# A routed mixture of experts dealt in two halves of the sequences, the first half's blocks between the steps of the second half's routing

## The chip, the cores and the metric

The kernel runs on one core of a Trainium2 chip. The metric is the device time of one execution in microseconds (us); the median over several runs counts. An engine's clock, where it is shown, is the TensorE clock granted by the throttle, as a share of full speed.

## The reference

Two decoder layers, six sublayers one behind another, each of the form x = x + f(layernorm(x)): attention, retention over a context, a mixture of experts; then attention with a rotation and a codebook, multi-query attention over the same context, and a second mixture of experts. x holds 32 sequences of 128 tokens of 256 floats, all in float32. The change is in the last sublayer:

```python
def _L1_ffn_ref(X, routing_W, expert_bias, sW1, sb1, sW2, sb2, rW1, rb1, rW2, rb2):
    E = 8
    K = 2
    ...
    shared = jax.nn.silu(X @ sW1 + sb1) @ sW2 + sb2
    logits = jnp.einsum('btd,ed->bte', X, routing_W) + expert_bias
    activation = jnp.sqrt(jax.nn.softplus(logits))
    top_vals, top_idx = jax.lax.top_k(activation, K)
    ...
    hdn = jax.nn.silu(jnp.einsum('nd,edh->enh', Xf, rW1) + rb1[:, None, :])
    y = jnp.einsum('enh,ehd->end', hdn, rW2) + rb2[:, None, :]
    routed = jnp.einsum('ne,end->nd', cf, y).reshape(B, T, d)
    return shared + routed
...
x = x + _L1_ffn_ref(_layernorm(x, axis=-1), ...)
```

Every token has a shared expert and its best 2 of 8 experts, each 256 to 128 to 256, weighted by the root of the softplus of their logits.

## The kernel before

The 128 tokens of a sequence lie on the 128 partitions. The 32 sequences stay in SBUF as x and are worked in 8 groups of 4 (r0 to r7 below are the routing objects of groups 0 to 7). The stages follow each other: A (attention), B (retention), C (first mixture), D with E (the second layer's two attentions, in 46 steps numbered -13 to 32, about 10 us each once the pipeline is full), a tail that ends the routing of the last mixture, F (its blocks), and the collecting of their results.

*Dealing by tables.* The routed expert work is done on sorted rows. For each group, `RouteF.norm` normalises x into a tile `f_h` (three buffers), `turn` transposes it, `choose` makes the logits, `rank` (`Dispatch.choose`) finds the two best experts and counts how many tokens each expert got so far, `place` works out each token's two rows in a table in HBM, `g_xs`, that has a region of 33 x 128 rows for each of the 8 experts, and `store` sends f_h's rows there: eight scatters a group, on POOL's queue (L329). A row carries its token's number with it. The regions are cleared ahead of that, in stage B, so that unwritten rows are marked. When all counts are known, `Dispatch.finish` (L362) works out by small operations on DVE which expert each block of 128 rows belongs to and where it starts. Blocks never cross an expert's region, so 64 full blocks' worth of rows need up to 71 blocks.

*The shared expert.* `hidden` (L596), `turn_shares` (L604), `shared` (L614, L618) of the same objects add the shared expert and the weighted output bias to x; `share` and `root` make the weights of the two experts (`r_wt`, on POOL, L584).

*What lies where.* In stage E a step works one sequence's scores on PE, with the reduction `e_pad` (L1423) on DVE, and carries the routing of earlier groups along at fixed lags. The routing of groups 0 to 4 is stored within the steps, together with the shared expert of groups 0 and 1. All the rest, the stores of r5, all of r6 and r7, `finish` and the shared expert of groups 2 to 7, is the tail (L1562 to L1601).

*Stage F.* It loads the experts' weights on SP (L1614, 2 MB), then works the 71 blocks: `read` fetches 128 rows from g_xs at an address held in a register (SP queue, issued 9 blocks ahead, 12 buffers), `turn` transposes them (L1635), `up` (L1645), `turn_hidden` (L1654) and `down` (L1660) are the expert, with copies from PSUM on DVE (L1650, L1665) and on ACT, `address` works out on DVE where each row's result belongs (L433, L438; `g_to` and `g_toi`, eight buffers), and `send` scatters the 128 result rows into a second table, `g_ys` (L329, POOL). A step of the loop holds turn of block j+4, up of j+3, turn_hidden of j+1, down of j and the address of j+2. On PE and SP the order of the code is kept as written; on the other engines a scheduler orders the instructions.

*Collecting.* After the loop 16 fetches (SP, L457) of 512 KB each bring the results of two sequences back, `collect` adds them on DVE with their weights (L466, four operations a fetch), and `store` writes the finished x on ACT's queue (L1693, 256 KB).

Of the kernel before, what the change touches and what calls it, by code (L numbers as in the profile page):

```python
# [22 lines left out]
F32 = mybir.dt.float32  # L23
# [19 lines left out]
NBLK = 2 * B + E - 1  # L43
# [3 lines left out]
REGION = (B + 1) * P  # L47


W = dict(r=D + 4, g=D + 2)  # L50
# [16 lines left out]
class K:  # L67
# [150 lines left out]
    def table(self, name, pool):  # L218

        self.tables[name] = (  # L220
            pool.tile([E * REGION, W[name]], F32, name=f"{name}_xs", tag=f"{name}_xs"),
            pool.tile([(NBLK + 2 * B) * P, D], F32, name=f"{name}_ys", tag=f"{name}_ys"),
        )

    def clear(self, name, e, behind=None):

        to = self.tables[name][0][e * REGION : (e + 1) * REGION, :].rearrange("(n p) w -> p n w", p=P)
        empty = self.empty[:, 0 : W[name]].unsqueeze(1).to_broadcast([P, REGION // P, W[name]])
        inst = self.nc.sync.dma_start(out=to, in_=empty).ins
        self.order(inst, behind)  # L230
# [18 lines left out]

class Dispatch:  # L250
# [5 lines left out]
    def __init__(self, k, name, p1, p2):  # L256
        nc = k.nc
        self.k, self.nc, self.p1, self.p2 = k, nc, p1, p2
        self.use(name)
        self.tri = self.tile([P, P], "tri")  # L260
        nc.sync.dma_start(out=self.tri, in_=k.ins["before"])
        consts = self.tile([P, E + NBLK + 2 * B + 1], "consts")
        nc.sync.dma_start(out=consts, in_=k.ins["cconst"])
        o = [0, E, E + NBLK, E + NBLK + B, E + NBLK + B + 1, E + NBLK + 2 * B + 1]
        self.region, self.blocks, self.starts, self.part, self.tok = (
            consts[:, a:b] for a, b in zip(o, o[1:])
        )
        self.ones = self.tile([P, P], "ones")
        nc.vector.memset(self.ones, 1.0)

        self.cum = self.tile([P, B + 1, E], "cum")
        nc.vector.memset(self.cum[:, 0, :], 0.0)

        self.spare = self.tile([P, NBLK], "spare")
        nc.vector.tensor_scalar(self.spare, self.blocks, float(P), self.part, ALU.mult, ALU.add)
        self.wt = self.tile([P, 2, B], "wt")

        self.down = self.tile([P, E], "down")
        nc.vector.tensor_scalar(self.down, self.blocks[:, 0:E], -1.0, float(E), ALU.mult, ALU.add)

    def use(self, name):

        self.name = name
        self.xs, self.ys = self.k.tables[name]

    def tile(self, shape, name, dtype=F32):
        return self.p1.tile(shape, dtype, name=f"{self.name}_{name}", tag=f"r_{name}")
# [6 lines left out]
    def choose(self, g, v, h, behind=None):  # L294


        nc = self.nc
        down = self.down.unsqueeze(1).to_broadcast([P, GB, E])
# [4 lines left out]
        for n in range(2):  # L303
# [15 lines left out]
            h[:, :, D + 1], h[:, :, D], 0.0, self.tok[:, g * GB : (g + 1) * GB], ALU.mult, ALU.add  # L319
# [3 lines left out]
        for i in range(GB):  # L323
            b = g * GB + i
            nc.vector.tensor_add(self.cum[:, b + 1, :], self.cum[:, b, :], self.both[:, i, :])
# [11 lines left out]
    def place(self, g, h):  # L337
        nc = self.nc
        pp = self.k.bank([P, GB, E])
        nc.tensor.matmul(pp, lhsT=self.tri, rhs=self.both, start=True, stop=False)  # L340
        nc.tensor.matmul(pp, lhsT=self.ones, rhs=self.cum[:, g * GB : (g + 1) * GB, :], start=False, stop=True)
# [20 lines left out]
    def finish(self):  # L362
        nc = self.nc

        pn = self.k.bank([P, E])
        nc.tensor.matmul(pn, lhsT=self.ones, rhs=self.cum[:, B, :], start=True, stop=True)
        count = self.tile([P, E], "count")
        nc.vector.tensor_copy(count, pn)
        need = self.tile([P, E, B], "need")
        nc.vector.tensor_tensor(  # L370
            need, count.unsqueeze(2).to_broadcast([P, E, B]),
            self.starts.unsqueeze(1).to_broadcast([P, E, B]), ALU.is_gt,
# [5 lines left out]
        for e in range(1, E):  # L378
# [5 lines left out]
        over = lambda v: v.unsqueeze(1).to_broadcast([P, NBLK, M])  # L384
        done = self.tile([P, NBLK, M], "done")
        nc.vector.tensor_tensor(
            done, over(end[:, 0:M]), self.blocks.unsqueeze(2).to_broadcast([P, NBLK, M]), ALU.is_le
        )
        self.be = be = self.tile([P, NBLK], "be")
        nc.vector.tensor_reduce(be, done, AX.X, ALU.add)  # L390
        self.bei = self.tile([P, NBLK], "bei", I32)
        nc.vector.tensor_copy(self.bei, be)
        picked = self.tile([P, NBLK, M], "picked")
        nc.vector.tensor_mul(picked, done, over(nb[:, 0:M]))
        br = self.tile([P, NBLK], "br")
# [5 lines left out]
        bc = self.tile([P, NBLK], "bc")  # L401
# [3 lines left out]
        self.bri = self.tile([P, NBLK], "bri", I32)  # L405
        nc.vector.scalar_tensor_tensor(self.bri, be, float(REGION), br, ALU.mult, ALU.add)
        self.regs = {}

    def load_regs(self, b0):
        why = "counts of tokens, held to the table's range by min and max on the chip"  # L410
        n = min(NREG, NBLK - b0)
# [6 lines left out]
            self.bri[0:1, b0 : b0 + n], engines=[mybir.EngineType.SP], min_val=0, max_val=E * REGION - P,  # L418
# [33 lines left out]
    def fetch(self, g, yg, first=0, n=GB):  # L452

        rows = 2 * P
        o = NBLK * P + (g * GB + first) * rows
# [3 lines left out]
    def collect(self, g, first, n, yg):  # L459

        self.fetch(g, yg, first, n)
        for i in range(n):
            x = self.k.x[g][:, first + i, :]
            for r in range(2):
                b = g * GB + first + i
                self.nc.vector.scalar_tensor_tensor(x, yg[:, i, r, :], self.wt[:, r, b : b + 1], x, ALU.mult, ALU.add)  # L466
# [9 lines left out]
class Route:  # L476
# [4 lines left out]
    def __init__(self, k, g, pool, behind=None):  # L481
# [1367 lines left out]
```

## Time and profile before

| | us |
|---|---|
| median of 3 runs | 1663.46 (1662.84 to 1666.61) |
| the profiled execution | 1662.12 |
| its span on the core | 1660.3 |
| PE busy in the span | 1451.6 |
| DVE, ACT, POOL busy | 927.1, 603.8, 594.4 |
| first send of the blocks (L329, g_ys) | starts at 1531.06 |
| last send of the blocks | starts at 1621.05 |
| first sum of the collecting (L466) | starts at 1628.03 |

Times in the profile count from the start of the span. Busy time of an engine does not hold register, branch, semaphore and DMA-issuing instructions. In a line of a group of instructions stand the source line, the engine, the operation, what it writes and reads, its count, its busy time and the mean of one in ns, then the idle time ahead of it and what ended most of that. The time line of the scatters, of POOL, at the beginning of the blocks reads:

```profile
1510.69 3.30 POOL L584 TENSOR_TENSOR r_wt<-f_s,half 128x8 f32<-128x8 f32 x2
...
1531.06 1.06 POOL L329 DMA_INDIRECT g_ys<-f_yb,g_toi  x1 [15.88 <-DVE g_to L433]
```

That is start, length, engine, line and operation; the brackets give the idle time ahead of it and what released it.

### The profile page before, as it was taken

Reading aid. Unit: us, or ns where it says so; the run is one execution under the profiler, and the core shown is the slowest. Engines: PE = TensorE matmul, PEld = TensorE weight load, DVE = VectorE, ACT = ScalarE, POOL = GpSimd, SP = SyncE. Lnnn points to the kernel's source line nnn. Section 1 sums busy time; section 2 is a strip of 40 time slices with the busy share of each in tenths; the row PEclk is TensorE's granted clock in tenths of the full one; section 3 lists DMA queues with packets and bytes.
Section 4 is the critical chain, followed back from the end, with each engine's and each line's share of the span. In section 5 each row is a group of like instructions: output and inputs, shape, how many; then the busy total and the mean of one; then the engine's idle time right before and its main releaser. Section 6 shows DMA issues by size and latency. Waiting matters only on the chain.

```text
span 1660.3 us, 26693 instructions
## 1 busy us (share of the span) xinstructions
PE 1451.6 (87%) x9166; PEld 965.0 (58%) x9166; DVE 927.1 (56%) x2944; ACT 603.8 (36%) x1528; POOL 594.4 (36%) x615
## 2 busy tenths in 40 slices
PE   6999799999998469999999995799999999877990
PEld 4555567777776336666666664365555555545870
DVE  7566447777778533333333323635667775645766
ACT  2544333343444012222222221135565554432550
POOL 2110136677778511111111113102223443345770
PEclk9999999999999579999999997769999988878995
DMA  9991199911000731111111115400000000023658
GB/s 337 335 336 42 35 303 305 277 34 40 28 27 30 314 137 48 45 45 45 45 45 46 48 33 189 150 5 9 3 1 8 27 26 27 27 102 109 205 173 316
DMA packets 130615, 180.93 MB, mean 109 GB/s; under 512 B 11690, under 2 KB 110964, under 8 KB 128436
## 3 DMA queue, kind: packets, MB, share of 16 engines
q1 hardware_dynamic: 112020, 138.21, 27.1%
q0 software_dynamic: 12960, 35.60, 6.0%
q10 hardware_dynamic: 5504, 5.43, 1.0%
q8 instruction: 76, 1.25, 0.3%
q14 instruction: 55, 0.45, 0.1%
HBM read 68.88 MB, written 110.32 MB: 108 GB/s over the span
## 4 chain that ended last, share of the span: by engine, by line
PE 72%; DVE 10%; POOL 5%; DMA 5%; ACT 4%; issue 2%; ACTq 0%; SPq 0%; POOLq 0%; DVEq 0%
PE ps L1016 15%; PE ps L1036 7%; PE ps L159 6%; PE ps L649 3%; PE ps L1398 2%; PE ps L1438 2%; PE ps L1416 2%; PE ps L241 2%; PE ps L1645 2%; PE ps L1029 2%; PE ps L1660 2%; DMA f_yg<-g_ys 2%; PE ps L863 2%; PE ps L879 2%; PE ps L154 2%
## 5 line engine op out<-in xcount | busy, mean ns | idle before, releaser
L1016 PE MATMUL ps<-c_wx,c_xT 128*128 x568 | 268.2, 595 | 0.0
L329 POOL DMA_INDIRECT r_ys<-c_yb,r_toi x71 | 68.1, 960 | 356.8 <-DVE r_w L446 316.5
L1016 PEld LDWEIGHTS ps<-c_wx,c_xT 128*128 128x128 f32 x568 | 102.9, 191 | 73.5 <-issue 69.9
L1036 PE MATMUL ps<-c_wx,c_hid 128*128 x568 | 134.8, 380 | 0.9 <-DVE c_hid L1031 0.9
L1036 PEld LDWEIGHTS ps<-c_wx,c_hid 128*128 128x128 f32 x568 | 107.4, 190 | 47.2 <-issue 18.4
L150 POOL TENSOR_TENSOR b_rs<-b_var,mhalf 128x16 f32<-128x16 f32 x32 | 93.5, 2923 | 76.5 <-DVE b_var L897 76.4
L869 DVE TENSOR_TENSOR b_sim<-ps,b_decay 128x512 f32<-128x512 f32 x128 | 79.4, 683 | 72.3 <-PE ps L863 72.3
L1041 ACT ACTIVATE c_yb<-ps,r_w 128x256 f32<-128x256 f32 x71 | 33.7, 474 | 219.3 <-PE ps L1036 219.3
L1031 DVE COPY c_hid<-ps 128x512 f32<-128x512 f32 x71 | 49.0, 691 | 101.2 <-PE ps L1029 101.2
L1423 DVE TENSOR_REDUCE e_pad<-ps 128x4 f32<-128x512 f32 x128 | 82.2, 681 | 10.3 <-PE ps L1416 10.3
L150 POOL TENSOR_TENSOR ln_rs<-ln_ve,mhalf 128x4 f32<-128x4 f32 x40 | 40.8, 1023 | 129.9 <-DVE ln_ve L178 129.8
L329 POOL DMA_INDIRECT g_ys<-f_yb,g_toi x71 | 68.3, 961 | 38.6 <-DVE g_to L433 18.3
L176 DVE BATCH_NORM_STATS2 ln_st<-x 128x6 f32<-128x256 f32 x192 | 74.8, 406 | 9.5 <-DMA x<-in_x_dram 5.4
L1024 DVE TENSOR_TENSOR c_su<-ps,c_su 128x512 f32<-128x512 f32 x71 | 49.1, 692 | 55.1 <-PE ps L1016 55.1
L1468 POOL TENSOR_TENSOR x<-x,e_t 128x256 f32<-128x256 f32 x32 | 23.2, 726 | 155.9 <-DVE e_t L1463 155.8
L1439 ACT ACTIVATE e_e<-ps 128x512 f32<-128x512 f32 x128 | 67.4, 603 | 27.0 <-PE ps L1438 26.8
L329 POOL DMA_INDIRECT r_xs<-c_h,r_rowi x64 | 64.3, 1005 | 27.5 <-issue 14.3
L1022 ACT ACTIVATE c_su<-ps 128x512 f32<-128x512 f32 x71 | 42.4, 597 | 86.2 <-PE ps L1016 86.2
L329 POOL DMA_INDIRECT g_xs<-f_h,g_rowi x64 | 62.7, 980 | 23.3 <-issue 14.7
L1416 PE MATMUL ps<-kp,e_qT 32*128 32x128 f32 x1024 | 67.0, 311 | 1.6 <-ACT e_e L1439 1.0
L1416 PEld LDWEIGHTS ps<-kp,e_qT 32*128 32x128 f32 x1024 | 52.4, 206 | 16.8 <-ACT e_e L1439 11.4
L446 DVE SCALAR_TENSOR_TENSOR r_w<-r_second,c_xb 128x1 f32<-128x1 f32 x71 | 15.6, 219 | 80.8 <-ACT c_yb L1041 80.8
(376 smaller groups left out, 3284.0 us busy)
## 6 DMA issues: line engine op xcount, KB each, us to landing
r_xs<-r_empty SPq DMA_DIRECT2D x8, 4290.0 KB
g_xs<-r_empty SPq DMA_DIRECT2D x8, 4257.0 KB
c_wx<-in_wx_dram SPq DMA_DIRECT2D x8, 1536.0 KB
c_xb<-r_xs SPq DMA_DIRECT2D x71, 130.0 KB
f_xb<-g_xs SPq DMA_DIRECT2D x71, 129.0 KB
c_yg<-r_ys SPq DMA_DIRECT2D x8, 1024.0 KB
f_yg<-g_ys SPq DMA_DIRECT2D x16, 512.0 KB
x<-in_x_dram SPq DMA_DIRECT2D x8, 512.0 KB
```

Source lines behind the costliest of these rows:

```text
L150: self.nc.gpsimd.tensor_tensor(out, in_, self.mhalf[: in_.shape[0], 0:n], ALU.pow)
L159: self.nc.tensor.matmul(out, lhsT=(xT[c] if isinstance(xT, tuple) else xT[:, c])[:, i * P : (i + 1) * P], rhs=w(c), start=c == 0, stop=c = ...
L176: self.order(nc.vector.bn_stats(st[:, i, :], x[:, i, :]).ins, behind)
L329: inst = self.nc.gpsimd.indirect_dma_start(out=table, out_offset=bass.IndirectOffsetOnAxis(ap=rows, axis=0), in_=src, in_offset=None,).ins
L649: nc.tensor.matmul(pk, lhsT=wA[:, c, w0 + f * P : w0 + (f + 1) * P], rhs=hT[:, c, :], start=c == 0, stop=c == NC - 1,)
L869: nc.vector.tensor_mul(self.sim[:, r].rearrange("p c s t -> p (c s t)"), ps[r].rearrange("p c s t -> p (c s t)"), decay[:, r].rearrange("p ...
L1016: nc.tensor.matmul(pu, lhsT=self.xT[:, c, :], rhs=weights(self.j, (2 * c + u) * FF0, FF0), start=c == 0, stop=c == NC - 1,)
L1024: nc.vector.tensor_mul(self.su, pu, self.su)
L1036: nc.tensor.matmul(py, lhsT=self.hid[:, f, :], rhs=weights(self.j, 2 * NC * FF0 + f * D, D), start=f == 0, stop=f == NF0 - 1,)
L1416: nc.tensor.matmul(ps[r][:, j, :], lhsT=self.group.qT[rows, j, self.i, :], rhs=self.keys[rows, :], start=True, stop=True,)
L1423: nc.vector.tensor_reduce(slots[:, :, r, HD], ps[r], AX.X, ALU.max, negate=True)
L1439: self.exp_by = nc.scalar.activation(self.e[:, r], ps, AF.Exp, scale=1.0 / 16.0).ins
```

## The change

The 32 sequences are dealt in two halves of 16, each with a `Dispatch` object of its own, tables of its own (`g0`, `g1`: regions of 17 x 128 rows) and 2 x 16 + 7 = 39 blocks, so 78 blocks in all. The constants that both share (`Deal`) are made once; a few tiles (region, tok, cum, be, bei, bri) exist for both. Stage B clears 16 regions rather than 8.

The first half's `finish` moves into step 27 of the attention. The experts' weights are loaded at step 20, into memory that the rotation's pool has given back by then (its operands have moved into that pool, and later pools lie on the right side of SBUF). The mean of the rotation is taken with a matrix of ones and a scale in the following copy, rather than with a matrix of 1/128.

The tail and the blocks become one interleaved order: `routing` walks through the routing and says after each piece how many steps of the blocks, `routed`, come next. 4 steps that only fill the pipeline lie ahead of `r7.place`, the steps of blocks 0 to 5 behind it and the second half's `finish`, 16 more between the pieces of the shared experts of groups 4 to 7, the other 56 behind. `r6.place` and r6's stores come directly behind `r7.turn`, ahead of `r3.hidden`. Once the first half's 39 blocks are done, its eight fetches, collects and stores lie among the steps: fetch m in step 41 + 4m, its sums in step 43 + 4m (kept behind that step's copy of the block's result), its store, on SP's queue, in step 45 + 4m. The other eight come at the end as before, with 6 buffers rather than 16 for the fetched results.

```diff
-    def __init__(self, k, name, p1, p2):
...
+    def __init__(self, k, name, first, n, p1, p2):
+        nc = k.nc
+        self.k, self.nc, self.name, self.first, self.n, self.p1, self.p2 = k, nc, name, first, n, p1, p2
...
+        self.nblk, self.rows = blocks(n), (n + 1) * P
...
-        o = NBLK * P + (g * GB + first) * rows
+        o = self.nblk * P + (g * GB - self.first + first) * rows
...
-        self.fetch(g, yg, first, n)
...
+                inst = self.nc.vector.scalar_tensor_tensor(
+                    x, yg[:, i, r, :], self.wt[:, r, b : b + 1], x, ALU.mult, ALU.add
+                ).ins
+                self.k.order(inst, behind)
...
-                        k.clear("g", e, load)
+                        for name in ("g0", "g1"):
+                            k.clear(name, e, load)
...
+    def operands(self, pool):
...
+                    routes[g - 1] = RouteF(k, g - 1, halves[(g - 1) * 2 // NG], pf, less_by)
...
+                if b == B - 5:
+                    halves[0].finish()
...
+                if b == B - 12:
+                    turns.close()
+                    experts = Experts(k, right.enter_context(tc.tile_pool(name="f2", bufs=1, side="right")))
                 step(b)
...
+class Experts:
+    def __init__(self, k, pool):
+        self.k, self.nc, self.pool = k, k.nc, pool
+        for name, shape in (("rw1", [P, E, NC, P]), ("rw2", [P, E, D]), ("rb1", [E, P])):
+            t = pool.tile(shape, F32, name=f"f_{name}")
+            k.nc.sync.dma_start(out=t, in_=k.ins[name])
+            setattr(self, name, t)
+        self.bias = {}
+    def biases(self, d):
+        nc = self.nc
+        hot = self.pool.tile([E, d.nblk], F32, name=f"f_hot_{d.name}", tag="hot")
+        nc.vector.tensor_scalar(hot, d.be[0:E, :], d.part[0:E, :], None, ALU.is_equal)
+        pb = self.k.bank([P, d.nblk])
+        nc.tensor.matmul(pb, lhsT=self.rb1, rhs=hot, start=True, stop=True)
+        self.bias[d] = self.pool.tile([P, d.nblk], F32, name=f"f_bias_{d.name}")
...
+        N = GB // 2
+        ygs = {}
+        def fetch(m):
+            g, h = divmod(m, 2)
+            ygs[m] = py.tile([P, N, 2, D], F32, name="f_yg")
+            halves[g * 2 // NG].fetch(g, ygs[m], h * N, N)
+        def collect(m, behind=None):
+            g, h = divmod(m, 2)
+            halves[g * 2 // NG].collect(g, h * N, N, ygs.pop(m), behind)
+        def routed():
+            AHEAD = 9
+            todo = [(d, j) for d in halves for j in range(d.nblk)]
+            half = len(todo) // 2
+            live = {n: Block(*todo[n]) for n in range(AHEAD)}
+            for n in range(-4, len(todo)):
+                if 0 <= n and n + AHEAD < len(todo):
+                    live[n + AHEAD] = Block(*todo[n + AHEAD])
+                for lag, what in ((4, "turn"), (3, "up"), (1, "turn_hidden"), (0, "down")):
+                    if 0 <= n + lag < len(todo):
+                        getattr(live[n + lag], what)()
+                last = live[n].last if n >= 0 else None
+                if 0 <= n + 2 < len(todo):
+                    live[n + 2].address(last)
+                live.pop(n, None)
+                for lag, what in ((2, fetch), (4, lambda m: collect(m, last)), (6, lambda m: store(k, nc.sync, m))):
+                    m, rest = divmod(n - half - lag, 4)
+                    if rest == 0 and 0 <= m < NG:
+                        what(m)
+                yield
+        def routing():
+            second = halves[1]
+            r5, r6 = r[NG - 3], r[NG - 2]
+            r7 = r[NG - 1] = RouteF(k, NG - 1, second, pf)
+            experts.biases(halves[0])
             for rest in range(GB):
-                last = r[NG - 3].store(rest)
-            r[NG - 3].root(last)
+                last = r5.store(rest)
+            r5.root(last)
             r[2].hidden()
             r[2].turn_shares()
             r6.choose(0)
...
             r6.rank()
             r7.norm()
             r[2].shared()
+            yield 0
             r7.turn()
+            r6.place()
+            for rest in range(GB):
+                last = r6.store(rest)
             r[3].hidden()
-            r6.place()
+            r[3].turn_shares()
+            yield 1
             r7.choose(0)
             r7.choose(1)
-            for rest in range(GB):
-                last = r6.store(rest)
             r7.rank()
-            r[3].turn_shares()
             r[3].shared()
-            r[4].hidden()
-            r[4].turn_shares()
+            yield 3
             r7.place()
             for rest in range(GB):
                 last = r7.store(rest)
-            k.disp.finish()
-            r[4].shared()
             r6.share()
             r7.share()
             r6.root(last)
             r7.root(last)
-            for g in range(5, NG):
+            second.finish()
+            yield 6
+            experts.biases(second)
+            for g in range(NG // 2, NG):
                 r[g].hidden()
-                if g > 5:
-                    r[g - 1].shared()
+                yield 1
                 r[g].turn_shares()
-            r[NG - 1].shared()
...
+                r[g].shared()
+                yield 3
         with tc.manual_schedule(engines={mybir.EngineType.PE, mybir.EngineType.SP}):
...
+            steps = None
+            for n in routing():
+                steps = steps or routed()
+                for _ in range(n):
+                    next(steps)
+            for _ in steps:
+                pass
+        for m in range(NG, 2 * NG):
+            fetch(m)
+            collect(m)
+            store(k, nc.scalar, m)
...
-        AHEAD = 9
         with tc.manual_schedule(engines={mybir.EngineType.PE, mybir.EngineType.SP}):
-            live = {j: Block(j) for j in range(AHEAD)}
...
-    with tc.tile_pool(name="fy", bufs=16) as p2:
-        for g in range(NG):
-            for h in range(2):
-                n = GB // 2
-                d.collect(g, h * n, n, p2.tile([P, n, 2, D], F32, name="f_yg"))
-                store(k, g, h)
```

## The prediction

> **What bounds the kernel now.** I began with the busy shares in 40 slices. TensorE is nearly full up to slice 35 and empty in the last one, where the DMA engines take over; the change works in the last five slices (41.5 us each), so I cut those by stage in the windows view: end of the attention, tail of the routing, the blocks, the collecting. Columns: PE, PEld, DVE, ACT and POOL busy (instructions), TensorE clock, DMA share, GB/s.
>
> ```profile
> 1420.00:1466.00 46.00, 39.71 (x238) 22.57 (x238) 27.52 (x111) 19.93 (x36) 13.40 (x17) 0.81 0.06 21
> 1466.00:1526.00 60.00, 43.15 (x183) 26.59 (x183) 31.09 (x152) 15.58 (x26) 34.49 (x41) 0.77 0.38 124
> 1526.00:1624.00 98.00, 87.92 (x640) 78.35 (x639) 65.72 (x282) 52.23 (x142) 68.26 (x71) 0.98 0.58 176
> 1624.00:1660.00 36.00, 0.00 (x0) 0.00 (x0) 26.31 (x64) 0.00 (x0) 0.00 (x0) 0.50 0.96 350
> 1540.00:1605.00 65.00, 63.69 (x469) 57.32 (x468) 48.36 (x208) 38.22 (x105) 48.39 (x51) 1.00 0.69 206
> 1626.00:1656.00 30.00, 0.00 (x0) 0.00 (x0) 25.19 (x62) 0.00 (x0) 0.00 (x0) 0.50 1.05 390
> ```
>
> No engine is full in the routing, PE is in the blocks (63.69 of 65.00), and the collecting is pure transfer. So each stage has a bound of its own, and the stages stand in a row. Then I read the chain of waits from 1460 (start, length, what):
>
> ```profile
> 1476.88 3.40 DMA g_xs<-f_h,g_rowi
> 1480.31 0.61 ACT f_h L193
> ...
> 1483.77 3.38 PE ps L596 x4
> ...
> 1509.72 0.96 POOL g_xs L329
> 1510.69 3.30 POOL r_wt L584 x2
> ...
> 1526.89 0.71 PE ps L1645 x4
> ...
> 1619.78 0.96 POOL g_ys L329
> 1621.05 2.40 DMA g_ys<-f_yb,g_toi
> ...
> 1632.09 7.62 DMA f_yg<-g_ys
> ```
>
> The tail waits for a scatter of group 4 to land before f_h has a buffer, then follows r7's scatters on POOL; the blocks run to the last send at 1621.05; the fetches take the rest, 39.25 us to the span's end at 1660.3. That execution took 1662.12, 1.8 more than its span, and the median 1663.46 is 1.3 above it.
>
> **The change, part by part.**
> (a) Load of the experts' weights, moved from the start of the tail into the attention, where DMA share is 0.06 of the window. In the tail it is issued on SP at 1470.62, just as r4's rows travel; at 390 GB/s its 2 MB are 5.4 us, about all of the 3.40 wait and more. Without it f_h is free some 4 us earlier (bounds 0 and 5.4), r7 turns and chooses 4 us earlier. r6.place now stands ahead of r3.hidden (3.38 at half clock), so r6's scatters start when POOL is done with r5's (1484) and not at 1490.65; 16 scatters of r6 and r7 at 1.27 each make 20.3, so r7's end near 1504.5, r_wt (3.3) and the first send at 1508. Before, it was at 1531.06.
>
> (b) The blocks are 78 instead of 71, and the sends, one per block on POOL, are 1.267 apart: 0.96 busy, 0.30 issue.
>
> ```profile
> L329 POOL DMA_INDIRECT g_ys<-f_yb,g_toi x71 | 68.3, 961 | 38.6 <-DVE g_to L433 18.3
> ```
>
> PE's step in this stretch is 1.21 (63.69 us hold 52 blocks), DVE's 0.96 (0.425 + 0.290 + 0.212 + 0.160, less overlap of records). Seven more blocks cost 7 x 1.267 = 8.9.
>
> (c) The dealing between routing and blocks. Four filling steps stand ahead of r7's placing and steps 0 to 5 behind it, in holes of PE (idle 16.9 of 60 in the routing window); DVE, which has the second half's finish() to do as well, carries them till about 1505. The next gate is the address of block 8: tiles of eight buffers, so it needs the first send landed, 1508 + 0.96 + 2.40 = 1511.4. Behind that wait on DVE stand the copies of block 7 and the sums of group 4, and PE waits for those. Then follow group 4's shared expert (about 3.4) and three steps (3.6): 1518.4. Groups 5 to 7 each cost hidden 1.72, share 0.27, the wait for ACT's transposed copy 0.41 and shared 0.71 + 1.95, in all 5.1, plus four steps of 1.21: 9.9 a group, 29.8 for three. Block 22 at 1548.2.
> The bounds of this stretch: POOL alone, 22 sends from 1508, gives 1537; three groups at half clock (3.4 more each for hidden) give 1558. I take 1548, as the clock stood at 1.00 wherever PE was fed as in the blocks. The row for the other state:
>
> ```profile
> 1480.00:1485.00 5.00, 3.99 (x10) 2.35 (x11) 1.26 (x9) 3.84 (x7) 3.68 (x6) 0.50 0.21 74
> ```
>
> That follows 6.4 us without PE work. The Trainium skill ("TensorE: Matmul & The Clock Gate", Part 1: The HAM clock gate) says that the clock falls to half after an idle window of about 3.4 us and comes back after a busy one; by it every 3.4 us hole that the dealing leaves would be paid for twice. The row agrees. The sum above leaves no such hole behind 1505.
>
> (d) finish() of the first half, some 30 small DVE instructions and one matmul, goes into step 27 of the attention. Its small operations stand between r4's rank and the last e_pad reduction, which PE waited for at 1420.10; they take about 4.4 (0.15 to 0.37 each, 0.2 apart overlapped). PE is 86% busy there, so part is caught up: I take +2, bounds 0 and 4.4. Block 22 at 1550. Against this, the finish() of the second half, 39 blocks, remains in the tail behind r7's scatters' rank and beside them on POOL: nothing.
> (e) Eight more table regions cleared in the retention stage (1.06 MB at 337 GB/s, 3.1 us of DMA): hidden by that stage's PE work; 3.1 if not. Two more register loads of 1.04 us on SP and PE: two PE holes, 2, in (c)'s bound. The POOL memset dropped (0.205) and the mean's scale in an activation: nothing.
> (f) From block 22 on POOL sets the pace: 55 x 1.267 plus one break of 1.3 as at 1616.95 makes 71: last send at 1621, as before.
> (g) Eight of sixteen fetches, collects and stores move among the steps 41 to 73. Per pair 786 KB. DMA: 0.69 x 1.267 = 0.874 a step, and 786 KB at 390 GB/s is 2.02 per four steps, 0.50: 1.38. DVE: 0.96 plus a sum of 0.40 each step: 1.36. Both pass POOL's 1.267 by about 0.11, so 32 x 0.11 = 3.5; I take +4 (bounds 0 and 12, the latter with the bytes at the blocks' own 206/0.69 = 299 GB/s and DVE and DMA out of step). The first fetch waits on SP for all sends of the first half, reads and stores queue behind it, and the reads have nine blocks of cover: +2 (0 to 4). Last send at 1627.
> (h) The tail then has eight pairs less: 39.25 - 8 x 2.02 = 23.1. Six buffers instead of sixteen hold 3 MB, at least 7.9 us of transfer: no loss.
>
> **Sum.** 1627 + 23.1 = 1650.1 span, +1.8 = 1651.9 against that execution's 1662.12, and +1.3 for the median: **1653**, -0.6%.
>
> **Rivals.**
> 1. *The transfers among the blocks fall behind* (slower side). Reads, sends, fetches and stores use the same DMA engines. The tail shows what a full set does: a fetch lands 7.62 to 7.87 after its predecessor with eight outstanding. A block's read is issued nine steps ahead and used by PE five steps later. If it lands after 7.87 plus one 512 KB fetch (1.34), 9.2 us, a step is 9.2/5 = 1.84; 32 x (1.84 - 1.267) = 18.3 in place of 4, and the first fetch's stall 4 in place of 2: 1669. No gain is left from a step of 1.72. For it: share 0.69 already. Against it: 1.38 is the mean demand, and twelve read buffers absorb a late fetch. The Trainium skill ("DMA: Bandwidth & Descriptors", Issuing engines are not separate DMA queues) says that issuing from another engine buys no new DMA engine, which speaks for this rival too: moving the stores from ACT's to SP's queue gives nothing. No trace here shows the stores on that queue.
> 2. *POOL is the bound from its first send.* PE hides group work better than the chain before showed (its holes there were waits for f_h and scatters): block 22 at 1537, **1640**. Against it: PE's work alone from 1484, 22 steps (26.6) and the shared experts of groups 3 to 7 (25.5), ends at 1536, so it may not leave one hole.
> 3. *The dealing lengthens the routing.* The filling steps on PE stand ahead of r7's placing, so what they wait for delays it: if r7's scatters end as before, at 1510.7, and each group finds PE cold, everything stands 11 later: **1664**, no change. For it: 0.77 of clock in that window.
> 4. *Collect and send exclude each other.* A sum with both inputs in SBUF never runs beside a send in this trace; if they took turns, POOL's step grew by 0.41 for 32 steps, 13.1 in place of 4: **1662**. The Trainium skill ("SBUF — State Buffer", SBUF: two separate sides) gives an exclusive lock between a DVE operation with two SBUF inputs and a GpSimd one that reads SBUF. Against it: g_toi has two SBUF inputs in each block, and sends stay at 0.96 to 1.06.
>
> **Chances.** Forecast 0.51 (its own range 1646 to 1659), rival 1 0.20, rival 2 0.10, rival 3 0.13, rival 4 0.06. About 0.2%, 3.3 us, is what a measurement can tell here. Faster: 0.51 + 0.10 + 0.03 of rival 3 and 0.02 of rival 4 = 0.66. Within: 0.07 + 0.04 = 0.11. Slower: 0.20 + 0.03 = 0.23. The range leaves out half of rival 2 below and half of rival 1 above: 1640 to 1668.
>
> **What would show it.** First g_ys send near 1508, r6's scatters from 1484, no wait of f_h for g_xs; block 22 near 1550; sends 1.27 apart outside, about 1.4 in, steps 41 to 73; last send near 1627; 23 us behind it. It is wrong if sends in those steps are over 1.7 apart (rival 1), 1.68 with POOL records stretched to 1.3 (rival 4), the first send comes after 1515 (rival 3), or the end of the attention is late by more than 4.4.

## The result, and the profile after

| | before | changed |
|---|---|---|
| median, us | 1664.48 (1662.84 to 1666.61, 4 runs) | 1650.10 (1648.07 to 1652.05, 4 runs) |
| ratio | | 0.9913, 95% interval 0.9895 to 0.9930 |
| profiled execution, its span | 1662.12, 1660.3 | 1648.07, 1645.9 |
| last residual of the attention starts (POOL, L1468, now L1488) | 1469.86 | 1471.32 |
| r7's f_h starts | 1480.31 | 1478.39 |
| first send | 1531.06 | 1509.75 |
| send of block 22 | 1560.34 | 1548.89 |
| last send | 1621.05 | 1622.72 |
| last send to the end | 39.25 | 23.18 |

The changed kernel is 14.4 us faster: 0.9% where 0.6% was forecast, at 1650.1 for 1653. Counted from the last residual within the profiled executions (one of each) it gains 15.9: 12.9 up to block 22 and 16.1 behind the last send, less 13.1 that the seven more blocks and the collects cost between the two. The same stages in the windows view of the changed kernel; its columns are those of the prediction.

```profile
1466.00:1513.00 47.00, 40.13 (x216) 29.05 (x215) 27.20 (x171) 20.28 (x41) 36.52 (x42) 0.89 0.46 142
1513.00:1546.00 33.00, 31.92 (x198) 24.75 (x199) 20.29 (x76) 13.03 (x36) 17.59 (x20) 1.00 0.43 133
1546.00:1575.00 29.00, 28.52 (x208) 25.32 (x207) 20.17 (x86) 16.99 (x47) 21.93 (x23) 1.00 0.64 186
1575.00:1623.00 48.00, 38.84 (x268) 33.27 (x266) 38.65 (x162) 22.02 (x60) 33.79 (x36) 0.97 0.88 293
1623.00:1645.90 22.90, 0.00 (x0) 0.00 (x0) 13.02 (x32) 0.00 (x0) 0.68 (x1) 0.50 0.81 285
```

The routing stretch, in which PE was busy for 43 of 60 us, is now 40 of 47. Then comes a stretch bound by PE (31.92 of 33, steps between shared experts), a stretch of pure blocks, a stretch in which the collects lie among the blocks and no engine is full though the DMA share is 0.88, and the transfer at the end. The chain of waits passes through the same places:

```profile
1473.51 4.73 DMA g_xs<-f_h,g_rowi
1478.39 2.08 ACT f_h L192 x4
...
1506.28 3.29 POOL r_wt L601 x2
1509.75 2.48 DMA g_ys<-f_yb,g_toi
1513.01 0.44 PE ps L1632 x2
...
1575.22 6.14 DMA f_yg<-g_ys
1581.94 0.47 DVE x L481 x2
...
1622.72 2.39 DMA g_ys<-f_yb,g_toi
1625.13 4.01 DMA f_yg<-g_ys
```

Three things are to be seen. f_h still waits for a scatter of r4, though the weights are no longer loaded there; its landing takes 4.73 us. The first send's landing is a link of the chain (1509.75 to 1512.23), the gate of step (c). And fetches have come into the chain in the middle of the blocks, where no fetch had been.

The two idle times behind these links, from the time lines of DVE and PE (start, length, engine, line, operation; in brackets the idle time ahead and what ended it):

```profile
1512.32 0.30 DVE L454 TENSOR_TENSOR g_toi<-g_to,r_spare 128x1 int32<-128x1 f32 x1 [4.42 <-DMA g_ys<-f_yb,g_toi]
...
1575.50 0.48 DVE L481 SCALAR_TENSOR_TENSOR x<-f_yg,r_wt,x 128x256 f32<-128x256 f32 x1 [2.14 <-DMA f_yg<-g_ys]
...
1581.38 0.48 DVE L481 SCALAR_TENSOR_TENSOR x<-f_yg,r_wt,x 128x256 f32<-128x256 f32 x1 [1.16 <-DMA f_yg<-g_ys]
```

```profile
1513.01 0.44 PE L1632 MATMUL ps<-ident,f_xb 128*128 128x128 f32 x2 [1.39 <-DVE x L639]
```

DVE stood still for 4.42 us at the gate, PE only for 1.39: the matmuls of group 4's shared expert were ahead of it. The sums wait for their fetch, which is issued only two steps earlier. The view of DVE's waits from 1570 to 1623 adds them up (total, times, longest):

```profile
DVE x L481 <- DMA f_yg<-g_ys: 6.8, 7, 2.1
```

### The profile page after: what moved, and what is told of

It is laid out like the page before. It is cut to its first block, busy times and chain, and to the rows that moved or that the text cites. A ratio compares the mean times of both kernels' runs of the same rounds, so it can differ in the third digit from the quotient of the medians.

```text
span 1645.9 us, 26941 instructions
## 1 busy us (share of the span) xinstructions
PE 1462.2 (89%) x9233; PEld 972.9 (59%) x9233; DVE 926.3 (56%) x3005; ACT 607.8 (37%) x1542; POOL 602.3 (37%) x621
## 3 DMA queue, kind: packets, MB, share of 16 engines
q8 instruction: 77, 1.26, 0.3%
## 4 chain that ended last, share of the span: by engine, by line
PE 69%; DVE 12%; POOL 5%; DMA 5%; issue 4%; ACT 4%; POOLq 0%; SPq 0%; DVEq 0%; ACTq 0%
PE ps L1034 13%; PE ps L1054 7%; PE ps L158 6%; PE ps L666 3%; PE ps L1418 2%; PE ps L1458 2%; PE ps L1436 2%; PE ps L241 2%; PE ps L881 2%; DMA f_yg<-g_ys 2%; PE ps L1047 2%; PE ps L897 2%; PE ps L153 2%; PE ps L840 2%; PE ps L822 1%
## 5 line engine op out<-in xcount | busy, mean ns | idle before, releaser
L344 POOL DMA_INDIRECT g_ys<-f_yb,g_toi x78 | 75.7, 971 | 37.0 <-DVE g_to L449 16.1
L175 DVE BATCH_NORM_STATS2 ln_st<-x 128x6 f32<-128x256 f32 x192 | 74.9, 406 | 10.5 <-DMA x<-in_x_dram 5.3
L1488 POOL TENSOR_TENSOR x<-x,e_t 128x256 f32<-128x256 f32 x32 | 23.2, 726 | 154.1 <-DVE e_t L1483 154.1
L344 POOL DMA_INDIRECT g_xs<-f_h,g_rowi x64 | 62.7, 980 | 18.7 <-issue 15.2
L1436 PEld LDWEIGHTS ps<-kp,e_qT 32*128 32x128 f32 x1024 | 52.2, 198 | 15.9 <-ACT e_e L1459 9.6
```

Source lines behind the costliest of these rows:

```text
L175: self.order(nc.vector.bn_stats(st[:, i, :], x[:, i, :]).ins, behind)
L344: inst = self.nc.gpsimd.indirect_dma_start(out=table, out_offset=bass.IndirectOffsetOnAxis(ap=rows, axis=0), in_=src, in_offset=None,).ins
L1436: nc.tensor.matmul(ps[r][:, j, :], lhsT=self.group.qT[rows, j, self.i, :], rhs=self.keys[rows, :], start=True, stop=True,)
```

## The experiments

They ran on three chips on which the kernel before takes 1705 to 1708 us, not 1664; the record gives no number for the chip of the first measurement, so that it is a fourth one is read from the times. So each is set against the kernel before on its own chip, and against the changed kernel there. Because the stages ahead of the tail vary by some us between executions, the last columns count within the profiled execution, one for each row, from the start of the attention's last residual on POOL. The ratios come with their intervals and need not be the quotients of the medians.

| run | chip | median, us | ratio to before (interval) | to first send | to block 22 | to the end |
|---|---|---|---|---|---|---|
| first chip, before | first | 1664.48 | | 61.20 | 90.48 | 190.44 |
| first chip, changed | first | 1650.10 | 0.9913 (0.9895 to 0.9930) | 38.43 | 77.57 | 174.58 |
| e2, same order as changed | second | 1697.60 | 0.9938 (0.9916 to 0.9959) | 41.85 | 90.03 | 207.34 |
| e1 | second | 1701.64 | 0.9956 (0.9936 to 0.9975) | 41.77 | 90.33 | 213.52 |
| e3 | second | 1701.82 | 0.9966 (0.9942 to 0.9989) | 57.02 | 94.99 | 212.41 |
| e4 | second | 1704.99 | 0.9984 (0.9972 to 0.9995) | 51.88 | 99.87 | 217.80 |
| a0, changed | third | 1698.76 | 0.9957 (0.9940 to 0.9973) | 44.33 | 90.85 | 209.00 |
| e5 | third | 1695.66 | 0.9951 (0.9934 to 0.9968) | 41.85 | 88.12 | 206.52 |
| e7 | third | 1695.02 | 0.9944 (0.9922 to 0.9965) | 41.80 | 89.80 | 209.80 |
| e8 | third | 1709.04 | 1.0018 (1.0004 to 1.0032) | 57.39 | 105.46 | 221.48 |
| b0, before | fourth | 1704.56 (one run) | | 61.48 | 99.12 | 218.69 |
| a1, changed | fourth | 1694.33 | 0.9941 (0.9917 to 0.9965) | 43.37 | 90.11 | 207.14 |
| e9 | fourth | 1696.59 | 0.9955 (0.9940 to 0.9971) | 40.18 | 88.85 | 206.11 |
| e10 | fourth | 1695.81 | 0.9946 (0.9927 to 0.9965) | 40.93 | 89.99 | 205.35 |

The same order of instructions needs 207.1 to 209.0 us to the end on these three chips, so differences of 2 us there say nothing; to block 22 it needs 90.0 to 90.9.

**The load of the weights (a).** e2 only writes the load behind the attention.

```diff
-                    experts = Experts(k, right.enter_context(tc.tile_pool(name="f2", bufs=1, side="right")))
...
+    experts = Experts(k, right.enter_context(tc.tile_pool(name="f2", bufs=1, side="right")))
     return routes, pf, experts
```

> The changed kernel with the load of the experts' weights back at the end of the attention, ahead of the reads of the blocks. Theory of the prediction: the load delays the landing of r4's last scatter, f_h of r7 comes 3 to 4 us later and so do r7's scatters, the first send and the end: 1653 to 1655. Rival: r7's scatters queue on POOL behind those of r5 and r6, which leave only 1.7 us of idle time there, and PE has other work to do: f_h moves by 3 to 4, the first send by 2 at most, the time by 0 to 2: 1650 to 1652.

Nothing held the load there, so the scheduler issued it at 1349.6, within the attention as before; all five engines have the order of the changed kernel. The run tells nothing of the load and serves as a measurement of the changed kernel on its chip. e8 has e2's edit and makes the load wait, by a copy on ACT from the last sequence's x into each of the weights' tiles:

```diff
+            one = {4: lambda: t[0:1, 0, 0, 0:1], 3: lambda: t[0:1, 0, 0:1], 2: lambda: t[0:1, 0:1]}[len(shape)]()
+            k.nc.scalar.copy(one, k.x[NG - 1][0:1, GB - 1, 0:1])
             k.nc.sync.dma_start(out=t, in_=k.ins[name])
```

> The changed kernel with the experts' weights loaded behind the last step of the attention: three copies of one element on ACT into the weights' tiles, from the last sequence's x, make the loads wait for it. Theory of the prediction, step (a): the loads travel beside r4's last rows, f_h of r7 gets its buffer 3 to 4 us later, and r7's scatters, the first send and the end follow: +3 to +4 us against the changed kernel. Rival: POOL's queue of scatters has 1.7 us of slack ahead of r7's and the blocks some more, so f_h moves by 3 to 4 and the end by 0 to 2.

Measured: 10.3 us above a0 in the median, 12.5 to the end, slower than the kernel before. f_h comes 2.9 us later (9.78 against 6.85 behind the residual), near what step (a) said, but the first send 13.1. Both theories miss that. PE's waits in the tail of e8, and the chain there:

```profile
PE ps L1608 <- issue: 14.4, 1, 14.4
```

```profile
1486.46 8.48 DMA f_rw<-in_rw_dram
1494.94 1.28 issue
1496.22 0.61 PE ps L1608 x2
```

L1608 (L1606 in the changed kernel) is the matmul that makes the first half's biases. It needs the small weight rb1, which is issued on SP right behind the 2 MB whose landing the chain names, and it stands first on PE, ahead of everything in the tail. The logits of r6 and r7 queue behind it, and their scatters behind those: POOL's longest hole was 13.2. So the early load is a condition of this order, which has brought a use of the weights to the head of the tail; f_h's buffer is the smaller part of the 12.5. No run moves this matmul further back, which might free the load's place again.

**The dealing (c).** e3 runs all routing and shared experts first, then the blocks, everything else as in the changed kernel.

```diff
-            yield 1
+            yield 0
...
-            yield 3
+            yield 0
...
-            yield 6
+            yield 0
...
                 r[g].hidden()
-                yield 1
                 r[g].turn_shares()
                 r[g].shared()
-                yield 3
```

> The changed kernel with its two halves, tables and collects among the blocks, but all routing and shared experts ahead of the first step of the blocks. Theory: the dealing fills PE's and POOL's holes in the routing, so without it the first send starts near 1529 as in the kernel before (less what f_h gains), 78 sends need 98.8 us, long steps 4, the end 23.2: span 1655 to 1657, time 1657 to 1660, 7 to 10 us above the changed kernel. Rival: PE has the same work in either order and is the bound, so the order matters little: 1650 to 1653.

The first send is 15.2 us later than in e2 on the same chip, block 22 only 5.0, the end 5.1; the median 4.2. The theory's place for the first send is right (57.0, as long behind the residual as 1544.41 is behind 1487.39), its price of 7 to 10 is too high, and the rival's 0 to 3 too low. The intervals of e2 and e3 overlap, so the 4.2 of the medians is not clear of noise; the 15.2 and the 5.0 are, by the spread of the changed kernel above. Most of what the first send gains is lost again in the stretch that PE bounds.

e9 moves only the four filling steps, from ahead of r7's placing to behind it.

```diff
-            yield 1
+            yield 0
             r7.choose(0)
...
-            yield 3
+            yield 0
             r7.place()
...
-            yield 6
+            yield 10
```

> The changed kernel with the four filling steps of the blocks moved on PE from ahead of r7's placing to behind it (ten steps there in place of six). Theory, rival 3 of the prediction: what the filling steps wait for holds up r7's placing and all that hangs on it (POOL sat idle for 7.6 us ahead of r7's first scatter in the run of the changed kernel on this kind of chip, 1.7 on the first one). Then r7's scatters and the first send come 4 to 6 us earlier where the hole is 7.6 (1 to 2 where it is 1.7), and the end 1 to 5 us. Rival: PE has the same work and the same waits in either order, and it is the bound to block 22: the first send moves, the end does not (within 1 us).

POOL's hole ahead of r7's first scatter, which the view of POOL's waits shows for a0 on the third chip in one line,

```profile
POOL g_xs L344 <- ACT f_xT L1634: 7.6, 1, 7.6
```

is gone in e9; no wait there is over 1.5 us. r7's last scatter comes 4.9 earlier than in a1 (34.08 against 38.93), the first send 3.2, block 22 1.3, the end 1.0, and the median is 2.3 above a1 with overlapping intervals. That is the rival's result, as far as one execution of each tells: the filling steps do hold up r7's placing where they wait, and PE takes most of it back. On the first chip the hole was 1.7.

**finish() of the first half (d).** e4 puts it at the head of the tail.

```diff
-                if b == B - 5:
-                    halves[0].finish()
...
+            halves[0].finish()
             experts.biases(halves[0])
```

> The changed kernel with finish() of the first half behind the attention, at the start of the tail, in place of step 27. Theory: its 30 small DVE operations stand ahead of r6's and r7's choosing, and the first reads, which need its result, leave SP about 8 us later; the first turn of a block on PE stands ahead of r7's logits and waits for its read, so r7's scatters and everything behind come 3 to 5 us later: 1653 to 1655. Attention not faster, as the changed kernel's step 27 cost nothing that can be seen there (its end is 0.2 us later than before). Rival: DVE and SP have slack in the tail, 1649 to 1651.

To the end 10.5 us more than e2, the median 7.4 above: the theory's direction, at twice its price. From the residual of sequence 26 to that of sequence 31, which holds step 27, e4 takes 57.39 and e2 57.42, so taking finish() out of step 27 saves nothing there. In the tail the reads do leave later, 9.4 us behind the residual (1490.77 behind 1481.40) and 0.8 in e2, but the first turn of a block on PE, at 1503.13, does not wait for them. PE's one wait from 1478 to 1500 is

```profile
PE ps L1604 <- issue: 9.8, 1, 9.8
```

L1604 is the matmul of the first half's biases again (L1608 in e8), first on PE in the tail. It needs the blocks' experts, which finish() works out, and starts 6.2 us behind the residual where it starts 3.9 ahead of it in e2 (1482.44 for 1486.36). r7's last scatter starts 10.0 us later than in e2, and the end is late by the same. So the theory's direction came by another path than the reads; e4 and e8 show the same instruction held up by two different operands.

**The collects (g).** e1 takes them out of the steps and writes all sixteen behind the blocks.

```diff
-                for lag, what in ((2, fetch), (4, lambda m: collect(m, last)), (6, lambda m: store(k, nc.sync, m))):
...
-        for m in range(NG, 2 * NG):
+        for m in range(2 * NG):
             fetch(m)
```

> The changed kernel with all sixteen fetches, collects and stores behind the blocks, none among them (16 at the end, through the same six buffers). Theory: the collects among the blocks cost about 4 us of longer steps and save eight pairs of 2.02 us at the end. Then all sends lie 1.27 apart behind block 22, the last one starts near 1618 to 1619 instead of 1622.7, the rest takes 39 us instead of 23.2, and the time is 11 to 13 us above the changed kernel: 1661 to 1663. Rival: the transfers among the blocks cost nothing, the long steps come from something else: the last send stays at 1622.7 and the time is 16 above, near 1666.

Neither happened. The first half has a table of its own, so nothing made its fetches wait for the second half, and the scheduler, which is free to move what the loop at the end writes, put them among the blocks again: eight fetches from 1608.07 on, eight stores, most sums one by one between the copies. The end of e1 is as short as that of the changed kernel, 23.25 us. It took 6.2 us more to the end than e2, 4.0 in the median, not clear of noise. What eight pairs at the very end would cost was therefore not measured; what shortens the end, by this run, are the tables of its own, with or without a place written for the collects.

e5 lets the sums follow their fetch by six steps.

```diff
-(4, lambda m: collect(m, last)), (6, lambda
+(8, lambda m: collect(m, last)), (10, lambda
```

> The changed kernel with the sums six steps behind their fetch in place of two (store two steps behind the sums as before). Theory: what the collects among the blocks cost is the wait of DVE for a fetch that was issued two steps, some 2.5 us, ahead and needs 4 to 6 us to land; with six steps (7.6 us) it has landed, DVE does not wait, and the long steps that lost 4.3 us behind block 22 are gone but for 0.1 a step: 3 to 4 us faster than the changed kernel. Rival 1 of the prediction, turned round: the DMA engines themselves are the bound there (share 0.90 in that stretch); then the waits only move to reads and stores, and the time is within 1 us of the changed kernel. Rival 4, DVE and POOL exclude each other: sends stay longer in the same number, no gain.

The median is 3.1 us below a0, but the intervals overlap, and the two executions that lie behind the last columns differ already at the first send, where the edit changes nothing. DVE's list of waits in a0 has no wait for a fetch among the blocks at all (on the first chip 6.8 us in seven waits), so what e5 takes away was not there on this chip. Whether it wins the 4 us on the first chip stays open.

e7 adds buffers to e5: ten for the addresses, out of a pool of the blocks, and nine for the results.

```diff
-        return self.p2.tile(
+        late = getattr(self, "late", None) if name in ("to", "toi") else None
+        bufs = 10 if late else 8 if name in ("to", "toi", "w") else 2
+        return (late or self.p2).tile(
...
-                yb = p3.tile([P, D], F32, name="f_yb", bufs=8)
+                yb = p3.tile([P, D], F32, name="f_yb", bufs=9)
...
+        for d in halves:
+            d.late = p3
```

> As the run before, and ten instead of eight buffers for the addresses of the results and nine instead of eight for the results. Theory: the address of block 8 no longer waits for the first send to land (DVE sat idle there for 4.4 us in the changed kernel, but PE only for 1.4, since it had group 4's work), so block 22 comes 1 to 1.5 us earlier, together 4 to 5.5 us faster than the changed kernel. Rival: PE catches up nothing, because POOL's queue sets the sends from the first one on: same as the run before.

Block 22 is not earlier (89.80; 88.12 in e5, 90.85 in a0), the median 0.6 below e5. But this run can't price the gate: neither a0 nor e5 has a wait of DVE for a send's landing, so the gate of block 8, seen with 4.42 us of DVE and 1.39 of PE on the first chip, does not hold anything up on this one. e10 has the edits of e9 and e5 together:

> As the run before, with the sums six steps behind their fetch as well. If both gains are real and independent, they add: 3 to 8 us faster than the changed kernel, ratio to the kernel before 0.990 to 0.994 where the changed kernel has 0.9945 to 0.996 (on the first chip 0.9913). Rival: within 1 us of the run before it.

It stands 1.5 us above a1, with overlapping intervals. No version was measured to be faster than the changed kernel clear of noise.

**Why the other chips gain less.** a0 and a1 are the changed kernel, b0 the kernel before.

> The changed kernel itself, as a base for the others on one chip. Expected: ratio to the kernel before 0.991 to 0.994, as in its first measurement (0.9913) and in the run with the weights' load merely written later (0.9938), whose instructions came out in the same order.

> The changed kernel itself on the chip of this batch, the base for the two runs before it. Expected 0.994 to 0.996 of the kernel before if the chip is like the last two, 0.990 to 0.993 if it is like the first.

> The kernel before, for its trace on the chip of this batch, because the two later chips gave 1706 to 1708 where the first gave 1664. Theory: there a block's step is longer than POOL's 1.267 (the changed kernel lost 25 us behind block 22 in steps of 2.3 to 3.1), so the seven more blocks cost 10 to 12 instead of 8.9 and the sends of the kernel before show the same long steps; its gain shrinks from 14 to 8 us for this reason. Rival: the kernel before keeps 1.27 a send there, and it is the change that brings the long steps.

The windows view of the kernel before, in the middle of its blocks, on the first chip and on the fourth:

```profile
1532.00:1620.00 88.00, 82.17 (x596) 73.07 (x594) 62.86 (x271) 48.91 (x133) 65.62 (x70) 1.00 0.62 189
```

```profile
1546.00:1656.00 110.00, 89.12 (x585) 74.57 (x584) 59.45 (x258) 44.06 (x130) 61.81 (x65) 0.97 0.48 146
```

70 sends in 88.0 us there, 65 in 110 here: 1.26 and 1.69 a send, with the same POOL time each (0.94 and 0.95). The long steps are the chip's, or its execution's, not the change's. But the expected reason for the smaller gain holds only in small part. From the residual to the end, the change gains 15.9 us on the first chip and 11.6 on the fourth (218.69 against 207.14). Behind block 22, seven more blocks and the collects cost 13.1 on the first chip (73.83 for 60.71) and 14.0 on the fourth (93.79 for 79.80); the seven blocks alone are 8.9 and 11.8, so the collects cost less where the steps are long. The shorter end gives 16.1 and 16.5. The difference is made ahead of block 22, which is 12.9 us earlier on the first chip and 9.0 on the fourth, and there already ahead of the first send: 22.8 earlier on the first, 18.1 on the fourth. The windows from the residual to the first send in the changed kernel, first chip and fourth (a1), and the ten us around that send in a1:

```profile
1471.32:1509.75 38.43, 33.13 (x176) 23.96 (x173) 24.73 (x157) 15.95 (x35) 29.71 (x32) 0.87 0.52 156
1484.96:1528.33 43.37, 29.00 (x157) 23.42 (x158) 24.52 (x150) 15.61 (x33) 30.04 (x32) 0.80 0.43 129
1525.00:1535.00 10.00, 8.23 (x21) 5.30 (x22) 2.90 (x13) 2.29 (x7) 8.83 (x13) 0.50 0.35 98
```

Up to the first send PE is not busy for 14 us on the fourth chip, in place of 5. The largest of its waits in a1 is for the filling steps' copies on ACT,

```profile
PE ps L1642 <- ACT f_xT L1634: 5.3, 2, 3.3
```

and what ACT waits for, the view does not tell. The granted clock in a1 is 0.50 from 1525 to 1535, though no hole of PE behind 1511 was over 2.8 us, and the hidden layer of group 4 takes 3.78 us there, from its first start to its last end, in place of 1.88. All of this stands on one execution for each kernel and chip.

## Why the prediction was right, step by step

The span was put at 1650.1 and was 1645.9, the median at 1653 and was 1650.1. Of the 4.2 us in the span 1.1 lie ahead of block 22, 1.3 in (f) and 1.7 in (g). Ahead of block 22 part of it is luck: the first send came 1.7 later than put, and (d) had 2 us too many.

**(a)** f_h 3.4 us earlier behind the residual, r6's scatters from 1484.86, r7's end 1506.27, the first send 1509.75: the figures hold within 2 us. So does the cause, though the sign that was named for it (no wait of f_h for g_xs) did not come, and though the row that the prediction read names a scatter that by its place is one of r5's. By the landings in the trace, the wait in the kernel before ended with the scatter issued at 1472.06, which landed at 1480.23, 8.2 us behind its issue and beside the 2 MB. In the changed kernel r4's last one is issued as long behind the residual (2.19 us, 2.20 before) and lands after 4.73, now beside twelve reads of the first blocks. What the list of waits did not hold is that the load's place also decides PE's first instruction in the tail; with f_h's share, that is 12.5 us in e8. A moved use has to be costed with what it stands ahead of, not only with what it waits for.

**(b)** 78 sends of 0.971 us, 1.267 apart wherever POOL set the pace.

**(c)** The gate at block 8 is there (DVE idle 4.42), its opening at 1512.23 was put at 1511.4, and PE's steps of 9.65 for groups 5 to 7 (1516.01, 1525.66, 1535.31 are their hidden layers' starts) were put at 9.9. Block 22 went at 1548.89 for 1550. None of groups 4 to 7 ran at half clock on the first chip: hidden took 1.72 each time. The Trainium skill's rule ("TensorE: Matmul & The Clock Gate", Part 1: The HAM clock gate) changed nothing here, since no hole behind 1505 came near 3.4 us. On the fourth chip group 4 did run at half clock (a1, above), behind holes of 2.8 us and less, so there the measurement does not follow the rule as it is stated. Two bounds were misworked: hidden at half clock is 3.38 for 1.72, so 1.7 more a group and not 3.4 (1553 and not 1558), and 22 sends of 1.267 from 1508 end at 1535.9 and not 1537. Rival 2 is refuted by the second window, where PE is full and POOL at 17.59 of 33.

**(d)** A mis-sized term: +2 forecast, nothing measured. The residual of sequence 28, after that step, starts at 1439.80, and at 1439.86 in the kernel before. PE's wait for e_pad in this step was 2.1 us before and is 1.8 now: the added small operations lay in time that DVE had. e4 says the same from the other side, and that the step's place is worth 10 us in the tail, as it has the biases' operand ready.

**(e)** The residual of sequence 0 is 0.9 later (1164.95 for 1164.01); with executions on one chip up to 4.8 us apart there (1170.44 to 1175.27 on the third), no run tells whether the clears are in it.

**(f)** No break of 1.3 came outside the collects, so 55 x 1.267 = 69.7 in place of 71. There was none in the kernel before either: its sends at 1615.99, 1617.25 and 1618.52 are 1.27 apart, and the piece at 1616.95 in the chain is the issue of one of them.

**(g)** The sum was +6 and 4.3 was measured, but its two terms were the wrong way round. The rate was costed at 1.38 a step by DVE and DMA share; between the waits the sends are 1.26 apart, at a DMA share of 0.88, so neither limits. What costs, by the place of the long sends, is latency: DVE waits for the fetch at seven of the eight sums, and the long sends, 2.59, 2.10, 2.19, 1.88 and three from 1.37 to 1.52, lie at sums. No run tests it, as e5 ran where these waits are missing. Only the first was in the sum, as 2 us: DVE waited 2.14 there, and the sends lost 1.3. That the two errors nearly cancel is luck.

**(h)** 23.1 forecast, 23.18 measured.

Rival 1 did not happen: the steps behind block 22 took 1.34 in the mean (73.83 us for 55), not 1.72, and the reads from 1577 to 1621 landed 4.0 us after their issue (median). Its 7.62 to 7.87 are times of one fetch from issue to landing, with others under way, and not the distance between two landings: the sums behind them start 1.9 to 2.0 apart. Rival 3's mechanism exists, as e9 shows and as group 4 at half clock in a1 does, but in e9 PE's work behind it covers most of what the hole costs. Rival 4 is refuted where a send and three sums lie side by side (POOL's and DVE's time lines, changed kernel):

```profile
1597.54 1.21 POOL L344 DMA_INDIRECT g_ys<-f_yb,g_toi  x1 [0.30 <-DVE g_to L449]
```

```profile
1597.91 1.27 DVE L481 SCALAR_TENSOR_TENSOR x<-f_yg,r_wt,x 128x256 f32<-128x256 f32 x3
```

The send covers 1597.54 to 1598.75 and the sums 1597.91 to 1599.18. Taking turns would have made one of them wait for the other's end; the send grew by 0.25 and the sums kept their 0.42 each. The Trainium skill's exclusive lock ("SBUF — State Buffer", SBUF: two separate sides) is stated for a GpSimd operation that reads SBUF, and by this row a scatter's issue is not held by it for a whole instruction.

## What to carry to other kernels

Interleaving two phases gains less than its first output does where one engine bounds what follows: in e3 against e2, a first send 15.2 us earlier became 5.0 at block 22. Once two phases share an in-order engine, look at which instruction of the second stands at the head of the first, since its operands must be there early (here one small matmul, held up by the weights in e8 and by finish() in e4, for 12.5 and 10.5 us to the end). A result that is fetched back would rather be used later than the fetch's landing time (4.0 to 5.8 us here) than as soon as the order of the code allows; no run here shows the gain. A table of its own is what frees the first half's fetch: e1 kept the short end without a place written for it.

## What was not expected of the hardware

The kernel before takes 2.5% longer on the three chips of the experiments. In b0, 28 of its 42 us more lie behind the attention, and there about every third send comes 2.6 us behind the one ahead of it in place of 1.27, at a granted clock of 0.97 and with sends of 0.95. From 1560 to 1640 PE's waits in b0 name ACT's f_hb (10.9 us), and ACT's name PE's transposes of the hidden layer (23.2). No view shows what both wait for; that stays open.
